# Keeping most nodes in place: a graph network's row permutation with four indirect transfers a batch in place of eight

## The chip, the cores and the metric

The kernel runs on one core of one Trainium2 chip. The metric is the device time of one execution in microseconds, the median of several runs. Engines are named as in the profile: PE (TensorE), PEld (its weight loads), DVE (VectorE), ACT (ScalarE), POOL (GpSimd), SP (SyncE, which here only issues DMAs, strictly in order).

## What is computed

Two layers on 16 batches of 1024 nodes with 128 features, and a 0/1 adjacency matrix per batch.

```
h = max(layernorm(x), 0)
x = x + layer0(h, adj)                       # masked dense attention
h = max(layernorm(x), 0)
x = x + layer1(h, adj, nodemask, ...)

layer0: v, q, k = relu(x W + b);  att = softmax(q k' masked by adj)
        relu(att v Wo + bo)
layer1: adj_d = dilate(adj)                  # sequential thinning of neighbours, node after node
        h1 = bn(relu(sage(h,  adj_d)))       # sage: deg-mean over adj_d, two matmuls, row norm
        h2 = bn(relu(sage(h1, adj_d)))       # bn: over all batches and nodes
        h3 = bn(relu(sage(h2, adj_d)))
        [h1, h2, h3] Wl + bl
```

After the thinning nearly all nodes have at most themselves or one neighbour left. The nodes with more to them are few: the "core" nodes (at most 128 a batch) keep a small matrix among themselves, the "special" ones (core included, at most 256) need a flag of their own. All other rows of adj_d are trivial.

## The kernel before, in words

The fast path (`fast`, L521) has five stages on one time line.

**Attention** (about 20 to 765 us). Sixteen steps of 48 ticks, one batch each; a tick is a third of a score block, and `pace` (L834) runs after each. Everything beside the score and value matmuls is written out by hand on the agenda (`plan_step`, L775): lists of tick numbers say when a generator's next piece is emitted. The pieces that matter here, by the step i in which they are emitted (list numbers of 48 and above fall into the following step):

- `load` (L158) for batch i+1: eight pairs, tile k at tick 1+6k. Each issues the DMA of 128 adjacency rows into one of three buffers `st` on SP and then ACT's exponential that reads them (L167); three ticks later ACT counts zeros (L184). The DMA and its reader are emitted at the same tick, so the lead that a load has over its use comes only from SP running ahead of the other engines, as far as free buffers allow.
- `load_x` (L666) at the start of step i brings x of batch i+2 into one of five buffers, the one that batch i-3 had. A column of the tile gets the node's number (L669).
- `sort` (L243) for a pair of batches in every odd step, ticks 27 to 36: it ranks core and special nodes and works out `slot` (a full permutation: core first, special next, then the rest) and `pick`.
- `gather` (L288): thirteen pieces a batch, for both batches of a pair, from tick 37 of the odd step to tick 46 of the next even one. Eight one-hot tiles, eight matmuls of one column (L300) for the core nodes' row numbers, then an indirect DMA of 128 adjacency rows on POOL (L305), a DVE scan over them (L309), and more.
- `norms_of_x2` (L706): the row norms of x after layer 0, ready around tick 22 of the second step after the batch's own; POOL writes the last of them (L586) into the x tile.
- `store` (L742): eight indirect DMAs of 128 rows of 524 bytes from POOL, which scatter x to `x2_d` in slot order, in the second step after the batch's own, ticks 27 to 41.

POOL further normalises x for the next projection (L592). In even steps that work and the newton steps of the norms stand ahead of the second batch's L305.

**Round one** (to 915 us): sage on the slot order. `load_x2` (L861) brings x2 back, POOL normalises (`enter`, L894), DVE solves the last four batches' thinning beside it. Batch 15's norms and store are emitted here.

**Round two** (to 990 us): sage again.

**Round three** (to 1119 us): sage, and the first two thirds of the last linear layer plus x2. The result rows of 11 of 16 batches have to go back from slot order to node order: `scatter_rows` (L1247) writes [h3 | z] with eight indirect DMAs of 1 KB rows to `y_d`, paced by `pace_scatters` (L1210), each behind a tiny POOL copy (L1217) that waits for recent DVE work; `load_back` (L1230) loads the rows three batches later. The other five (`STAY`) stay in slot order.

**The end** (from 1119 us): batch norm three, the last third (`final`, L1302), and the output: one dense store for the 11, eight indirect scatters (L1292) for each of the five.

All indirect DMAs are issued from POOL, all dense ones from SP. Each queue is in order, and a wait holds whatever is behind it.

## Time and profile before

| | us |
|---|---|
| median of 3 runs (1195.01 to 1197.49) | 1195.18 |
| the profiled execution | 1192.21 |
| its span, first to last instruction | 1190.4 |

| stretch, us | PE busy | DVE | ACT | POOL | DMA share | GB/s |
|---|---|---|---|---|---|---|
| 30 to 740, attention | 657.43 | 514.75 | 516.72 | 315.38 | 0.41 | 122 |
| 765 to 800, into round one | 25.30 | 22.15 | 13.81 | 25.70 | 0.40 | 107 |
| 800 to 915, round one | 85.84 | 99.72 | 66.45 | 64.97 | 0.18 | 48 |
| 915 to 990, round two | 64.77 | 62.27 | 51.60 | 5.99 | 0.05 | 12 |
| 990 to 1119, round three | 121.62 | 92.28 | 42.18 | 92.66 | 0.71 | 213 |
| 1119 to 1190.4, the end | 49.94 | 27.98 | 13.88 | 47.93 | 0.56 | 168 |

The DMA share is the mean busy share of the core's 16 DMA engines; it can exceed 1 where packets overlap. In attention, odd steps take 43.5 to 45.3 us with 0 to 0.8 us of PE idle (from step 3 on), even ones 47 to 53 us with 4.6 to 7.8.

| DMA | issues | median us from issue to landing |
|---|---|---|
| adjacency tile to `st`, SP | 128 | 3.6 |
| x tile, SP | 16 | 4.5 |
| x2 back, SP, round one / round three | 16 / 16 | 4.0 / 6.2 |
| x2 scatter, POOL | 128 | 2.8 |
| y scatter, POOL | 88 | 3.5 |
| adjacency rows gather, POOL | 16 | 4.6 |
| y back, SP | 22 | 5.8 |
| out, dense, SP | 11 | 4.0 |
| out, scatter, POOL | 40 | 2.4 |

### The profile page before, as it was taken

The numbers are of one execution on the slowest core, as the hardware profiler recorded it, in microseconds if no ns is written. First come the engines' busy times: TensorE is split into PE (matmuls) and PEld (weight loads), VectorE is DVE, ScalarE is ACT, GpSimd is POOL, SyncE is SP. The second block draws the span as 40 slices with busy tenths as digits, with TensorE's granted clock in tenths as the row PEclk, the third lists the DMA queues.
The fourth block names the chain that finished last, engine by engine and source line by source line (L and its number), as shares of the span: only waits on it lengthen the run. The fifth ranks groups of instructions, "written<-read, shape, count | busy, mean of one in ns | idle before, by whom it ended". The sixth has DMA issues, their size and how long they took to land.

```text
span 1190.4 us, 22335 instructions
## 1 busy us (share of the span) xinstructions
PE 1049.6 (88%) x7693; PEld 815.7 (69%) x7723; DVE 860.0 (72%) x2627; ACT 727.7 (61%) x1658; POOL 566.7 (48%) x1063
## 2 busy tenths in 40 slices
PE   7799899899889989989989989878876997999794
PEld 3567677667667666757656657667765997999784
DVE  6767656677777767867867877868887886777742
ACT  5578688677768868767767765246654772333221
POOL 0320743644445346356165270589740101878775
PEclk9999999999999999999999999989899998999897
DMA  6544345344344443543424431243300002788764
GB/s 212 159 130 142 103 129 149 107 127 143 102 121 113 150 124 96 159 124 104 146 87 130 139 104 24 58 109 86 96 1 1 1 1 74 237 246 248 219 195 132
DMA packets 135340, 143.78 MB, mean 121 GB/s; under 512 B 25904, under 2 KB 111280, under 8 KB 135216
## 3 DMA queue, kind: packets, MB, share of 16 engines
q1 hardware_dynamic: 123312, 111.10, 32.5%
q0 software_dynamic: 11904, 31.15, 8.0%
q8 instruction: 63, 1.03, 0.4%
q14 instruction: 61, 0.50, 0.1%
HBM read 113.71 MB, written 28.51 MB: 119 GB/s over the span
## 4 chain that ended last, share of the span: by engine, by line
PE 50%; DVE 22%; POOL 8%; ACT 7%; DMA 6%; issue 5%; POOLq 0%; SPq 0%; DVEq 0%; ACTq 0%
PE ps L714 11%; PE po L730 10%; PE pm L693 6%; PE po L1000 5%; DMA rows<-in_adj_dram,row 4%; DVE e L717 4%; PE pt L1058 2%; DVE left L309 2%; PE ph L1242 2%; ACT e L716 2%; PE pd L193 2%; PE ph L1243 2%; DVE m L366 2%; PE pm L701 2%; POOL out_dram L548 2%
## 5 line engine op out<-in xcount | busy, mean ns | idle before, releaser
L730 PEld LDWEIGHTS po<-vw,e 128*128 128x128 f32 x2048 | 271.8, 193 | 64.9 <-issue 64.5
L730 PE MATMUL po<-vw,e 128*128 128x129 f32 x2048 | 305.6, 283 | 0.0
L714 PE MATMUL ps<-qT,kT 128*128 128x512 f32 x512 | 270.0, 610 | 0.8 <-ACT e L716 0.8
L717 DVE TENSOR_TENSOR e<-e,ab 128x512 f32<-128x512 f32 x256 | 177.4, 694 | 120.7 <-ACT e L716 119.3
L716 ACT ACTIVATE e<-ps 128x512 f32<-128x512 f32 x256 | 152.8, 597 | 102.3 <-PE ps L714 78.5
L548 POOL DMA_INDIRECT x_d<-xt,slot x128 | 143.1, 1118 | 38.3 <-issue 34.9
L167 ACT ACTIVATE ab<-st,d_one_k 128x1024 bf16<-128x1024 f32 x128 | 146.9, 1148 | 1.2 <-DMA st<-in_adj_dram 1.2
L580 POOL TENSOR_SCALAR ln_t<-ln_st 128x8 f32<-128x8 f32 x31 | 7.7, 248 | 289.9 <-DVE ln_st L573 234.6
L184 ACT ACTIVATE junk<-st 128x1024 bf16<-128x1024 f32 x112 | 118.2, 1056 | 0.0
L548 POOL DMA_INDIRECT y_d<-y,nodes x88 | 86.3, 981 | 18.1 <-issue 13.3
L739 ACT ACTIVATE o<-po,recips 128x128 f32<-128x128 f32 x128 | 46.7, 367 | 77.2 <-DVE recips L737 77.2
L1016 ACT ACTIVATE sq<-po 128x512 f32<-128x512 f32 x64 | 38.1, 597 | 78.1 <-PE po L1035 43.5
L714 PEld LDWEIGHTS ps<-qT,kT 128*128 128x128 f32 x512 | 78.4, 192 | 7.5 <-issue 3.1
L592 POOL TENSOR_SCALAR hn<-xt,ln 128x128 f32<-128x128 f32 x120 | 73.8, 626 | 1.6
L309 DVE TENSOR_TENSOR_SCAN left<-rows 128x1024 f16<-128x1024 f32 x16 | 36.6, 2289 | 46.4 <-DMA rows<-in_adj_dram,row 46.4
L199 DVE SCALAR_TENSOR_TENSOR junkv<-pd,ab 128x64 bf16<-128x64 int32 (+7 forms) x128 | 57.6, 450 | 15.1 <-PE pd L193 15.0
L1000 PE MATMUL po<-ws,r 128*128 128x128 f32 x512 | 68.3, 278 | 0.0
L237 PEld LDWEIGHTS <-ab 128*128 128x128 bf16 x448 | 26.4, 97 | 60.7 <-issue 60.1
L592 POOL TENSOR_SCALAR hn<-xt 128x128 f32<-128x128 f32 x112 | 57.0, 518 | 22.7 <-PE pt L602 21.8
L1000 PEld LDWEIGHTS po<-ws,r 128*128 128x128 f32 x512 | 65.6, 195 | 1.1
L1019 DVE TENSOR_REDUCE nrm<-sq 128x4 f32<-128x512 f32 x64 | 43.5, 681 | 22.4 <-ACT sq L1016 22.1
L305 POOL DMA_INDIRECT rows<-in_adj_dram,row x16 | 17.1, 1068 | 83.0 <-DVE row L303 56.5
(330 smaller groups left out, 2414.0 us busy)
## 6 DMA issues: line engine op xcount, KB each, us to landing
st<-in_adj_dram SPq DMA_DIRECT2D x128, 512.0 KB, 3.6
r<-y_d SPq DMA_DIRECT2D x22, 512.0 KB, 5.8
xt<-x_d SPq DMA_DIRECT2D x16, 524.0 KB, 4.0
xt<-in_x_dram SPq DMA_DIRECT2D x16, 512.0 KB, 4.5
x<-x_d SPq DMA_DIRECT2D x16, 512.0 KB, 6.2
out_dram<-r SPq DMA_DIRECT2D x11, 512.0 KB, 4.0
x_d<-xt,slot POOLq DMA_INDIRECT x128, 2.8
y_d<-y,nodes POOLq DMA_INDIRECT x88, 3.5
```

Source lines behind the costliest of these rows:

```text
L167: nc.scalar.activation(ab[:, k, :], st, AF.Exp, bias=self.one_k, scale=ONE_K, accum_out=self.deg[:, b, k:k + 1])
L184: nc.scalar.activation(junk(), st, AF.Exp, scale=-ZERO_K, accum_out=zeros)
L199: nc.vector.scalar_tensor_tensor(junk.rearrange("p a b -> p (a b)")[:, :n], pt.rearrange("p a b -> p (a b)").bitcast(I32)[:, :n], 1.0, ab[ ...
L309: nc.vector.tensor_tensor_scan(left[:, ::-1], rows[:, ::-1], rows[:, ::-1], 0.0, op0=OP.add, op1=OP.bypass)
L548: d = nc.gpsimd.indirect_dma_start(out=dst, out_offset=bass.IndirectOffsetOnAxis(ap=slots, axis=0), in_=src, in_offset=None)
L592: engine.tensor_scalar(hn[:, k, :], xt[:, k, :D], minus[:, k // 2, k % 2, None], rstd[:, k // 2, k % 2, None], op0=OP.add, op1=OP.mult)
L693: nc.tensor.matmul(pp, w, hT[:, 512 * g:512 * g + 512], start=True, stop=True)
L714: nc.tensor.matmul(p, K[b][:, k * P:(k + 1) * P], Q[b][:, c], start=True, stop=True)
L716: later(1, lambda: nc.scalar.activation(e, p, AF.Exp))
L717: later(2, lambda: nc.vector.tensor_mul(e, e, AB_[b][:, k, c]))
L730: nc.tensor.matmul(po[:, q % 2, :], E[k][:, i * P:(i + 1) * P], V[b][:, k, :], start=(k == 0), stop=(k == NB - 1))
L1000: nc.tensor.matmul(po[:, i, :], hT[:, c:c + P], wxk, start=(i == 3), stop=False)
```

## The change

Slots are assigned anew. Core and special nodes still occupy the first slots of the first two blocks (256 slots). A node that is neither stays where it is, except where its own place in the first two blocks is needed: such a displaced node goes to the place that a special node from further behind has left. Blocks 2 to 7 are then nearly the natural order.

- `sort` computes `pick` for 256 slots, and for the displaced nodes of the first two blocks whom they change with; twelve small operations of that run on POOL.
- `gather` computes the node numbers of all 256 slots: the eight matmuls have 256 columns, and four DVE operations read their columns out.
- `store` becomes a dense DMA of the tile in node order (SP), two indirect fetches of the 256 special rows from there, two indirect scatters of the displaced rows of blocks 0 and 1 (POOL), and a dense DMA of the fetched rows over the first two blocks (SP). The node number column is gone.
- Round three sends batches 0 to 8 home: a dense store of y (SP), two fetches by `slot`, two scatters by `source` (POOL), and two loads of blocks 2 to 7 (SP). x2 is loaded into the y tile, which now has four buffers. The paced copies are gone.
- The end takes the seven batches 9 to 15 first, which are still in slot order: each a dense store to `y_d` and one to `out` (blocks 2 to 7), two fetches, two scatters of special rows to `out`, a dense store of blocks 0 and 1. Batches 0 to 8 follow with one dense store each. Three batches are transposed and raised before the last batch norm, not one.

```diff
-STAY = (2, 5, 8, 11, 14)
+HOME = 9
-XW = D + 3
+XW = D + 2
...
         nc.tensor.matmul(pp[:, 1, :, :, 0], self.onesb, count, start=True, stop=True)
+        for k in range(2):
+            nc.tensor.matmul(pp[:, 1, :, :, 1], self.onesb, kind[:, :, :, k], start=(k == 0), stop=(k == 1))
         yield
...
+        g = nc.gpsimd
+        g.tensor_sub(gone, other, stays)
...
+        g.tensor_mul(skip, skip, self.spare[:, None, :].to_broadcast([P, 2, 2]))
+        self.displaced[b0] = with_, where
         yield
...
-        pi = self.bank([P, 1], F32)
+        ph = self.bank([P, S], F32)
         for k in range(NB):
-            nc.tensor.matmul(pi, onehot[:, k, :P], self.node16[:, k:k + 1], start=(k == 0), stop=(k == NB - 1))
+            nc.tensor.matmul(ph, self.node16[:, k:k + 1].to_broadcast([P, P]), onehot[:, k, :],
+                             start=(k == 0), stop=(k == NB - 1))
         yield
+        def column(i):
+            nc.vector.scalar_tensor_tensor(line[:, :P], ph[:, i * P:(i + 1) * P], 1.0, self.identf, op0=OP.mult,
+                                           op1=OP.mult, accum_out=home[:, i:i + 1])
+        column(0)
         row = self.pool.tile([P, 1], I32, name="row")
...
         nc.gpsimd.indirect_dma_start(out=rows, out_offset=None, in_=self.adj.rearrange("b n m -> (b n) m"),
                                      in_offset=bass.IndirectOffsetOnAxis(ap=row[:, 0:1], axis=0))
+        column(1)
+        with_, where = (t[:, b % 2] for t in self.displaced[b - b % 2])
+        for k in range(2):
+            nc.vector.scalar_tensor_tensor(line, self.iota, with_[:, k:k + 1], ph, op0=OP.is_equal, op1=OP.mult,
+                                           accum_out=home[:, 2 + k:3 + k])
...
         def store(b):
-            for k in range(NB):
-                scatter(x2_d[b], dil.slot[:, b, k:k + 1], X[b][:, k, :], f"x2_{b}")
+            natural = x2_d[b][:N].rearrange("(k p) d -> p k d", p=P)
+            nc.sync.dma_start(natural, X[b])
+            yield
+            special = dpool.tile([P, 2, XW], F32, name="special")
+            for k in range(2):
+                fetch(special[:, k, :], x2_d[b][:N], source[:, b, k:k + 1])
                 yield
+            for k in range(2):
+                scatter(x2_d[b], away_to[:, b, k:k + 1], X[b][:, k, :], f"x2_{b}")
+                yield
+            nc.sync.dma_start(natural[:, :2, :], special)
             X.pop(b)
+            yield
...
-        AT_STORE = every(75, NB, 2)
+        AT_STORE = [78, 84, 85, 91, 92, 95]
-        LAST_NORMS, LAST_STORE = [42, 44, 46, 48, 50], every(54, NB, 2)
+        LAST_NORMS, LAST_STORE = [42, 44, 46, 48, 50], [53, 58, 59, 64, 65, 68]
...
+            def send_home(b, y):
+                there = y_d[b].rearrange("(k p) d -> p k d", p=P)
+                put(2, lambda: nc.sync.dma_start(there, y))
+                for k, to in enumerate((tall(b), r1[b // 2][:, b % 2, :])):
+                    put(7 + k, lambda k=k, to=to: fetch(to[:, :2 * D], y_d[b], slot[:, b, k:k + 1]))
+                    put(12 + k, lambda k=k: scatter(y_d[b], source[:, b, k:k + 1], y[:, k, :], f"y_{b}"))
+                def back():
+                    for i, rows in enumerate((rows_r, rows_z)):
+                        nc.sync.dma_start(rows(b)[:, 2:, :], there[:, 2:, i * D:i * D + D])
+                put(19, back)
...
+        def send_out(b):
+            there = y_d[b].rearrange("(k p) d -> p k d", p=P)
+            rows = rows_z(b)
+            def dense():
+                nc.sync.dma_start(there, rows)
+                leave(nc.sync.dma_start(places[b][:, 2:, :], rows[:, 2:, :]), b)
...
+            put(2, dense)
+            for k in range(2):
+                put(6 + k, lambda k=k: fetch(rows_r(b)[:, k, :], y_d[b], slot[:, b, k:k + 1]))
+                put(8 + k, lambda k=k: special(k))
+            put(13, lambda: leave(nc.sync.dma_start(places[b][:, :2, :], rows_r(b)[:, :2, :]), b))
...
-        order = [b for i in range(0, B - 1, 3) for b in (i + 2, i, i + 1)] + [B - 1]
+        order = list(range(HOME, B)) + list(range(HOME))
```

`put(n, fn)` runs `fn` n ticks later, where a round-three batch has eight ticks and a batch of the end four. `fetch` is an indirect DMA on POOL that reads rows by number.

## The prediction

> **What bounds the kernel now.** I read the slices first, then the waits by engine, then single stretches in order of time.
>
> ```profile
> PE   7799899899889989989989989878876997999794
> POOL 0320743644445346356165270589740101878775
> DMA  6544345344344443543424431243300002788764
> ...
> L548 POOL DMA_INDIRECT x_d<-xt,slot x128 | 143.1, 1118 | 38.3 <-issue 34.9
> ```
>
> A slice is 29.8 us. PE is full for 25 slices (attention and dilation, 30 to 740 us: PE 657 of 710), POOL only in round three and the end (last seven digits). So the scatters that the change thins out in attention (L548, 143.1 us) stand on an engine with room; their saving is worth nothing there unless somebody waits for POOL.
>
> What does matter there is the order of the SP queue:
>
> ```profile
> SPq L166 <- ACT junk L184: 338.6, 79, 8.1
> SPq L668 <- DMA x_d<-xt,slot: 149.4, 30, 18.9
> ```
>
> SP stands still most of the time: for a free adjacency buffer (L166) and, at each step's end, for the last scatter, so that the next x can be loaded (L668). It is in order; whatever is put between waits like these delays all loads after it. One pair of steps (i = 8, 393.1 to 440.5 us, and i = 9, to 484.1), SP, POOL, ACT and PE in turn:
>
> ```profile
> 405.82 0.33 SPq L166 DMA_DIRECT2D st<-in_adj_dram  x1
> 474.48 0.38 SPq L668 DMA_DIRECT2D xt<-in_x_dram  x1
> 475.59 2.16 SPq L166 DMA_DIRECT2D st<-in_adj_dram  x2
> ...
> 415.61 0.21 POOL L586 TENSOR_TENSOR xt<-ln_t 128x8 f32<-128x8 f32 x1
> 418.22 1.06 POOL L305 DMA_INDIRECT rows<-in_adj_dram,row  x1 [0.15 <-issue]
> 461.60 0.22 POOL L586 TENSOR_TENSOR xt<-ln_t 128x8 f32<-128x8 f32 x1
> ...
> 415.63 1.14 ACT L167 ACTIVATE ab<-st,d_one_k 128x1024 bf16<-128x1024 f32 x1
> 484.06 1.15 ACT L167 ACTIVATE ab<-st,d_one_k 128x1024 bf16<-128x1024 f32 x1
> ...
> 416.83 1.62 PE L602 MATMUL pm<-identf,hn 128*128 128x128 f32 x4 [1.00 <-POOL hn L592]
> 428.98 1.13 PE L693 MATMUL pm<-hT,w_L_gnn_Wk 128*128 128x512 f32 x2 [1.95 <-ACT qT L694]
> ```
>
> The load of tile k=5 leaves at 405.82, ten us ahead of its use (ACT, 415.63); tile k=0 of the next batch leaves at 475.59, 8.5 us ahead (484.06). L586 on xt (415.8, 461.8) is when the row norms that are stored with x are ready.
>
> The end is POOL's:
>
> ```profile
> 1131.44 0.95 POOL L548 DMA_INDIRECT out_dram<-r,nodes  x1 [0.30 <-issue]
> ...
> 1180.67 0.96 POOL L548 DMA_INDIRECT out_dram<-r,nodes  x1 [0.30 <-issue]
> ```
>
> Forty scatters without a gap, (1180.67-1131.44)/39 = 1.262 us each; PE is done at 1174.1. The last lands about 2.4 us after its issue (median of that row), 1183.1; the rest to 1190.4 is the closing.
>
> **A: the dense store of x, middle of an even step.** It stands at tick 30, right before the load of k=5 (tick 31), and needs the norms. In step 8 it can leave at 415.8 only, so k=5 leaves at 416.2 and not at 405.8. In front of it are 532 KB: at 300 GB/s (round three moved 213 GB/s at a DMA share of 0.71) 1.8 us. An adjacency load lands in 3.6 us, so k=5 lands at 421.6, and ACT holds from 415.6: 6 us, with the exps, the hT and qT evictions behind it, and PE behind these. But PE and DVE already stand there for the rows gather (418.22, landed 422.8, DVE idle 6.24 us before its scan); I follow ACT's list after the hold (hT, e, junk, qT: 4 us) and it is through at about 426, when today's o eviction starts (426.1). What is left is the rows' own delay: 512 KB that now share the engines with the store and three loads let go at once, at most 1.6 us at half rate (0.52 MB at E's 320 GB/s); 1.3, because its first part goes before them. Ends: 0 and 5.7 a step. I take 1.3, seven even steps: **+9**.
>
> **B: the start of the step after an odd one.** The chain is now dense store, two fetches, two scatters, each behind the landing of the one before. Store 461.8, landed 466.5. But on POOL the new sort's 12 small operations (tick 33) come ahead of the fetches (tick 36); their inputs come from DVE at about 470.5 (the operations they replace end at 470.0), and at 0.28 us each (0.20 and a gap of 0.08, the ln_t rows) they end at 474. Fetches 474 and 475.3; landed 2.8 later (median of x_d), 478; scatters 478 and 479.3, landed 482.2. Today the last scatter lands at 474.4. SP holds the patch of 133 KB, the load of x, the diagonal and k=0 until then: 8 us later, against a lead of 8.5 of which the landing behind the x load takes some 5.5. ACT is held 4 to 5 us. Scores stop two PSUM buffers later, so I count 2.5 (ends 0 and 5.4). Leads of the five such loads are 8.4 to 10.1; the sixth (12.6) has room: **+12.5**. In even steps POOL has nothing between, and the chain ends at about 429, earlier than today's 432.8.
>
> **C: PE and DVE in the gather.** Eight 128x1 matmuls (L300, 0.18 us together) become eight 128x256 (L324's shape, 0.87): +0.69. In even steps PE idles 4.6 to 7.8 us anyway; odd steps have at most 0.8 of idle, so seven times 0.69: **+5**. The four new DVE operations (dg's row, 0.34 and 0.08 for 128x128; twice that at most for 256) are 0.4 ahead of the rows gather and 1.7 behind it, hidden in DVE's wait for the rows, in odd steps in B's hold; without that cover 1.7 x 16 = 27.
>
> **D: into round one.** load_x2(2) left at 761.1; it now stands behind batch 14's store (norms at 778.6) and its patch. The chain of B from 778.7: landed 783, fetched by 787, scatters landed at 791.5. Then the load, 4.0 to landing: 795.5. On POOL two normalisations of batch 2 (L592, 791.69) come before batch 15's rows gather, at 792.73 today, then at 796.7: 4 us later on the chain that leads through DVE. Ends 0 and 4.3; I take **+3.5**. Thinner POOL work in round one (four transfers fewer, no node numbers, L898 0.24 each) hides behind PE and DVE; so does L669's copy (0.17) that falls away in attention.
>
> **E: round three.** 88 scatters (1.36 us with their mark) become 36 indirect transfers; POOL goes free. That gives 1.6 us: turns follow each other at 7.33 us, fourteen of them from 1008.49 would end at 1111.1 and end at 1112.70. Against that, a home batch now moves 0.5 MB (x2), 1.05 (y out), 0.26 + 0.26 and 0.79 (back): 2.88 MB, nine in a row; at 320 GB/s (what loaded stretches of eight us show) 9.0 us against PE's 7.33. Before it was 2.62 MB in two batches of three. The four y buffers come free when the scatters land, and load_rows stands ahead of the next dense store in SP, so lateness adds up: 9 x 1.7 = 15, less some 5 of slack in the early loads, less the 1.6. Ends -1.6 and +13; I take **+6**.
>
> **F: the end.** Three raises before the last batchnorm put four more evictions (0.6 us each) ahead of its Sqrt: +1.3. First dense store about 1130.7, landed 1134.8; then POOL 28 x 1.262 = 35.4 us. The last fetch starts at 1166.4 and lands at 1169. PE is done earlier (two raises fewer after the norm and four moved ahead), at about 1170, but SP's order puts batch 15's patch before the out stores of the last seven natural batches; they leave in a burst: 3.8 MB at 300 GB/s, 12.7 us, and about 2 more to land: 1184.5 against 1183.1. Ends -8 (no hold: last store 1171, landed 1175) and +5: **+1.5**.
>
> Sum: 9 + 12.5 + 5 + 3.5 + 6 + 1.5 = 37.5. The profiled execution took 1192.2 (span 1190.4), 3.0 below the median 1195.2, so 1229.7 for such an execution and 1195.2 + 37.5 = 1232.7 for the median, **1232** in round numbers.
>
> The Trainium skill speaks against the plan on one point: DMA: Bandwidth & Descriptors, "Issuing engines are not separate DMA queues", says that DMAs of all issuers run on the same 16 engines and that another issuer saves sequencer time alone. Round three's rows agree (share over 1 with both queues at work), and by the rule E would be its upper end. The page's "Anatomy of one DMA" (told there for GpSimd's path) puts a DMA at 2.0 us and bytes over 436e3; as an estimate the dense store of B would land after 3.2 us, not 4.7, which would make B's hold 1.5 us shorter and the sum some 5 us less.
>
> **Rivals.** R1, faster: the end alone counts. If SP's new waits stay inside the loads' lead (A, B, D at 0) and batch 15's patch isn't waited for long (F -8), with E at -1.6: 1195.2 - 9.6 = 1185.6. For it: loads lead by 10 to 20 us in most places, and POOL's gapless end. Against it: the two leads above are the short ones, and the patch is in order. It decides if k=5 lands before 416 and k=0 before 484. R2, attention absorbs, the rest costs: C, E, F and a third of A and B: 5 + 6 + 1.5 + 7 = 1215. R3, holds paid nearly in full: A 4 and B 5 a time, D 4, E 10, C, F: 28 + 25 + 4 + 10 + 5 + 2 = 1269. That it doesn't do what it says: the transfers are written out one by one, I give it nothing.
>
> **Chances.** Forecast 0.55 (own range 1222 to 1245), R2 0.20, R3 0.12, R1 0.13. 1192 to 1264 leaves R1 and half of R3 out. 0.2% is what a measurement of this kernel can tell from no change. Faster 0.13, same 0.04 (between R1 and R2), slower 0.83.
>
> **What would show it.** ACT's L167 idle before, by st's landing, where it is 7.9 us in all today: about 60. Steps after odd ones longer by 3 to 5. rows of batch 15 at 797. PE idle in round three's first nine batches. SP's last out stores in a burst behind a fetch. Wrong if the steps keep their 43.5 and 47 to 53 us.

## The result and the profile after

| | before | after |
|---|---|---|
| median, us (same chip, 4 runs each) | 1195.1 | 1296.02 |
| ratio after to before (95% interval) | | 1.0843 [1.0821, 1.0865] |
| span of the profiled execution, us | 1190.4 | 1295.0 |
| start to the first bn_aggr (attention, dilation, round one) | 915.6 | 991.5 |
| round two | 73.5 | 73.4 |
| round three | 130.9 | 156.5 |
| the end | 70.4 | 73.6 |

Slower, as predicted, but by 101 us and not by 37, beyond the range's 1264. The spans of the two profiled executions differ by 104.6: 75.9 of it up to the end of round one, 25.6 in round three, 3.2 in the end. (The borders are the three starts of DVE's bn_aggr, one a batch norm.)

The slices of the changed kernel's page, 32.4 us each:

```profile
PE   7899798898899799889789889857876979878792
PEclk9999899999999899889889989978998999988996
DMA  7534435335333443353433441143500014888077
```

PE is no longer full in attention, and the granted clock (PEclk) falls below 9 in 9 of its first 28 slices, where that of the kernel before does in one. The DMA row has hardly changed: attention has not become a matter of bytes alone.

The waits by engine of the changed kernel (sum in us, times, longest):

```profile
ACT ab L171 <- DMA st<-in_adj_dram: 84.9, 19, 8.1
...
DVE left L354 <- DMA rows<-in_adj_dram,row: 78.6, 8, 13.9
...
SPq L807 <- DMA x_d<-xt,moves: 208.8, 16, 19.5
SPq L798 <- DVE xt L630: 159.1, 13, 27.3
SPq L170 <- ACT junk L188: 147.2, 39, 8.0
```

In this row ACT's wait for adjacency tiles was 1.2 us before (the prediction's 7.9 has the first tile of the kernel in it, 6.7). SP used to stand for free buffers, ahead of everybody (L166, 338.6); now it stands in front of the patch (L807, the dense DMA that puts the fetched rows into the first two blocks) and the dense store (L798), with the loads behind it. DVE's wait for the gathered rows went from 46.4 to 78.6.

One even step (i = 8, 423.4 to 475.5 us), SP, ACT and PE in turn:

```profile
415.59 0.38 SPq L807 DMA_DIRECT2D x_d<-special  x1
416.02 0.72 SPq L722 DMA_DIRECT2D xt<-in_x_dram  x1
...
417.78 11.83 SPq L170 DMA_DIRECT2D st<-in_adj_dram  x5
...
446.22 0.38 SPq L798 DMA_DIRECT2D x_d<-xt  x1
446.70 2.20 SPq L170 DMA_DIRECT2D st<-in_adj_dram  x3
...
423.36 1.15 ACT L171 ACTIVATE ab<-st,d_one_k 128x1024 bf16<-128x1024 f32 x1 [4.77 <-DMA st<-in_adj_dram]
...
452.60 1.15 ACT L171 ACTIVATE ab<-st,d_one_k 128x1024 bf16<-128x1024 f32 x1 [6.02 <-DMA st<-in_adj_dram]
...
425.14 2.07 PE L767 MATMUL ps<-qT,kT 128*128 128x512 f32 x2 [3.81 <-ACT e L769]
454.38 1.67 PE L746 MATMUL pm<-hT,w_L_gnn_Wq 128*128 128x512 f32 x2 [3.54 <-ACT hT L657]
```

At its start the patch lets go of SP at 415.6, the load of k=0 goes at 417.8, ACT stands 4.77 us for it (this is B), PE 3.81 for ACT's e. In its middle the dense store waits for the norms until 446.2, k=5 goes half a us later, ACT stands 6.02 (this is A) and PE 3.54 for ACT's hT, the transposed h that ACT brings out of PSUM for the next projection.

In the table, steps run from ACT's L171 (L167 before) on k=0 of one batch to that of the next; "even" is the sum of steps 2, 4 to 12, "odd" of 3, 5 to 13. Since B delays that mark itself, the two columns share B between them, and their sum is the safe number.

| kernel | even | odd | PE idle in both | clock, even | step 14 to bn_aggr | time | ratio to before |
|---|---|---|---|---|---|---|---|
| before | 297.1 | 265.1 | 36.7 | 0.983 | 240.2 | 1195 | |
| after | 317.1 | 309.2 | 68.2 | 0.907 | 250.8 | 1296.0 | 1.0843 |
| b_dense | 324.3 | 267.4 | 52.9 | 0.947 | 244.5 | 1226.9 | 1.0258 [1.0223, 1.0292] |
| b_small | 312.9 | 264.5 | 41.9 | 0.951 | 242.5 | 1213.2 | 1.0143 [1.0109, 1.0177] |
| b_wide | 303.2 | 268.8 | 30.8 | 0.949 | 242.8 | 1204.8 | 1.0070 [1.0042, 1.0099] |
| a_late | 303.6 | 306.8 | 56.2 | 0.916 | 249.8 | 1285.7 | 1.0772 [1.0717, 1.0826] |
| a_patch | 324.9 | 272.9 | 50.2 | 0.942 | 251.9 | 1272.8 | 1.0629 [1.0592, 1.0667] |
| a_warm | 328.6 | 272.3 | 44.1 | 0.964 | 255.3 | 1277.0 | 1.0683 [1.0643, 1.0722] |
| a_x2early | 314.6 | 309.0 | 67.9 | 0.918 | 246.1 | 1291.6 | 1.0795 [1.0751, 1.0839] |
| a_three | 311.5 | 272.3 | 41.5 | 0.951 | 249.1 | 1261.5 | 1.0564 [1.0527, 1.0601] |
| a_six | 312.4 | 273.1 | 43.3 | 0.956 | 245.0 | 1229.6 | 1.0299 [1.0254, 1.0343] |

Clock is the granted clock as a share of full speed. Times are medians of several runs, stages those of one execution each, and these vary: seven executions with the changed kernel's attention untouched reached the first bn_aggr between 988.9 and 996.4 us, and six with its round three untouched took 152.9 to 160.0 us there. A smaller difference in one stage of one execution is no finding by itself.

### The profile page after: what moved, and what is told of

The parts are those of the page before. It is cut to its first block, busy times and chain, and to the rows that moved or that the text cites. A ratio compares the mean times of both kernels' runs of the same rounds, so it can differ in the third digit from the quotient of the medians.

```text
span 1295.0 us, 22232 instructions
## 1 busy us (share of the span) xinstructions
PE 1090.6 (84%) x7693; PEld 839.9 (65%) x7723; DVE 881.5 (68%) x2758; ACT 723.5 (56%) x1654; POOL 447.0 (35%) x957
## 3 DMA queue, kind: packets, MB, share of 16 engines
q8 instruction: 62, 1.02, 0.3%
## 5 line engine op out<-in xcount | busy, mean ns | idle before, releaser
L783 PEld LDWEIGHTS po<-vw,e 128*128 128x128 f32 x2048 | 280.1, 199 | 72.3 <-issue 71.6
L783 PE MATMUL po<-vw,e 128*128 128x129 f32 x2048 | 313.8, 288 | 0.1
L767 PE MATMUL ps<-qT,kT 128*128 128x512 f32 x512 | 278.5, 628 | 28.8 <-ACT e L769 28.8
L171 ACT ACTIVATE ab<-st,d_one_k 128x1024 bf16<-128x1024 f32 x128 | 147.1, 1149 | 84.9 <-DMA st<-in_adj_dram 84.9
L767 PEld LDWEIGHTS ps<-qT,kT 128*128 128x128 f32 x512 | 81.6, 200 | 36.8 <-ACT e L769 32.0
L354 DVE TENSOR_TENSOR_SCAN left<-rows 128x1024 f16<-128x1024 f32 x16 | 36.8, 2302 | 78.6 <-DMA rows<-in_adj_dram,row 78.6
L646 POOL TENSOR_SCALAR hn<-xt,ln 128x128 f32<-128x128 f32 x120 | 73.5, 626 | 1.6
L600 POOL DMA_INDIRECT r<-y_d,moves x32 | 31.2, 975 | 114.1 <-DVE r L1136 52.3
L1301 PE MATMUL ph<-ws,r 128*128 128x128 f32 x256 | 54.1, 295 | 5.3 <-DVE y L1136 2.8
L746 PE MATMUL pm<-hT,w_L_gnn_Wq 128*128 128x512 f32 x60 | 37.2, 705 | 24.9 <-ACT hT L657 24.9
L593 POOL DMA_INDIRECT x_d<-xt,moves x32 | 39.7, 1239 | 49.6 <-DMA special<-x_d,source 42.0
```

Of the source, the lines that this page charges most:

```text
L171: nc.scalar.activation(ab[:, k, :], st, AF.Exp, bias=self.one_k, scale=ONE_K, accum_out=self.deg[:, b, k:k + 1])
L593: d = nc.gpsimd.indirect_dma_start(out=dst, out_offset=bass.IndirectOffsetOnAxis(ap=slots, axis=0), in_=src, in_offset=None)
L646: engine.tensor_scalar(hn[:, k, :], xt[:, k, :D], minus[:, k // 2, k % 2, None], rstd[:, k // 2, k % 2, None], op0=OP.add, op1=OP.mult)
L767: nc.tensor.matmul(p, K[b][:, k * P:(k + 1) * P], Q[b][:, c], start=True, stop=True)
L783: nc.tensor.matmul(po[:, q % 2, :], E[k][:, i * P:(i + 1) * P], V[b][:, k, :], start=(k == 0), stop=(k == NB - 1))
L1301: nc.tensor.matmul(pz[:, i, :], r1[b // 2][:, b % 2, c], wl0, start=True, stop=False)
```

## The experiments

### Attention: each cost alone, on the kernel before

**b_dense**, A alone:

```diff
...
+        def dense(b):
+            nc.sync.dma_start(x3_d[b].rearrange("(k p) d -> p k d", p=P), X[b])
+            yield
...
                 plan(store(i - 1), start, LAST_STORE if last else AT_STORE)
+                if not last:
+                    plan(dense(i - 1), start, [78])
```

> The kernel before, with A alone: one dense store of x with its norms (520 KB) on SP at the changed kernel's place (tick 78 of its store's step, right before the load of k=5), into a buffer that nothing reads; the eight scatters stay. Theory 1 (the order of SP's queue holds the adjacency loads, and the whole hold reaches PE): ACT's ab idle by the landing of st rises from 8 us to 40 or more, at k=5 of the even steps, even steps are longer by about 3.3 each, odd ones by at most 0.5, time 1195 + 23 = 1218. Rival (the hold is hidden in the wait for the rows gather, as the prediction had it): ACT's idle rises as much, but the steps lengthen by 1.3 at most, time 1200 to 1204. Rival 2 (it is the bytes, not the order): odd steps lengthen as much as even ones.

Measured 30 us, of it 27.2 in the six even steps and 2.3 in the odd ones: one DMA costs three times the nine that the prediction gave it, and more than the 23 that theory 1 expected. (The eight scatters stay here, so its 520 KB come on top of what the kernel before moves.) Its waits:

```profile
DVE left L309 <- DMA rows<-in_adj_dram,row: 77.8, 9, 12.5
...
ACT ab L167 <- DMA st<-in_adj_dram: 59.5, 14, 8.5
...
PE pm L694 <- ACT hT L604: 25.9, 7, 4.4
```

The last line is the one that the prediction had ruled out: PE's projection of the next batch waits for ACT's hT, which stands behind the held ab. The kernel before has no such row. Two causes are mixed here, ACT's hold and the rows that land late.

**b_small** takes them apart: the same place in the queue, 65 KB.

```diff
...
-            nc.sync.dma_start(x3_d[b].rearrange("(k p) d -> p k d", p=P), X[b])
+            nc.sync.dma_start(x3_d[b], X[b][:, 0, :])
```

> The kernel before with b_dense's extra store cut to one of eight row groups (65 KB in place of 520), at the same place of SP's queue and behind the same norms, into a buffer that nothing reads. Order theory (the loads behind it are let go late, ACT is held): ab's idle stays at 50 or more us, time 1195 + 25 = 1220, as b_dense's 1227. Bytes theory (520 KB beside the rows gather and three loads make all of them land late): the wait of DVE for the rows falls from 78 back to 46 or so, time 1195 to 1206.

```profile
DVE left L309 <- DMA rows<-in_adj_dram,row: 66.4, 9, 11.0
...
ACT ab L167 <- DMA st<-in_adj_dram: 40.2, 8, 7.4
...
PE pm L694 <- ACT hT L604: 16.7, 7, 3.3
```

Between the two theories: 17 us with an eighth of the bytes. At this place in the queue 17 of A's 30 come with a store of any size, and 13 with the rest of the 520 KB.

**b_wide**, C alone:

```diff
-        pi = self.bank([P, 1], F32)
+        ph = self.bank([P, S], F32)
...
-            nc.tensor.matmul(pi, onehot[:, k, :P], self.node16[:, k:k + 1], start=(k == 0), stop=(k == NB - 1))
+            nc.tensor.matmul(ph, self.node16[:, k:k + 1].to_broadcast([P, P]), onehot[:, k, :],
+                             start=(k == 0), stop=(k == NB - 1))
...
```

> The kernel before, with C alone: in each of the 16 gathers eight matmuls 128x256 in place of eight 128x1, and DVE's diagonal read ahead of the rows gather and three reads behind it, whose results beyond the row are not used. Prediction's C: 7 x 0.69 = +5, time 1200. Rival (cover is gone, since DVE's 1.7 us behind the gather and a later row count in every step): 16 x (0.7 + 1.7) = +38, time 1233. Rival (all of it hidden): 1195.

Ratio 1.0070, 8.4 us: C was 5 in the prediction. The even steps, where it was to be hidden in PE's idle time, took 6.1 of the 9.8 in the table. PE's idle time there did fall (35.5 to 30.0 us), but its busy time rose by 11.6: 4.1 of work by the prediction's price (six times 0.69), the rest with a granted clock of 0.949 in place of 0.983.

### Attention: each cost taken away, on the changed kernel

**a_late**, the store of even steps behind k=6:

```diff
-        AT_STORE = [78, 84, 85, 91, 92, 95]
+        AT_STORE = ([78, 84, 85, 91, 92, 95], [86, 89, 90, 93, 94, 95])
...
-                plan(store(i - 1), start, LAST_STORE if last else AT_STORE)
+                plan(store(i - 1), start, LAST_STORE if last else AT_STORE[odd])
```

> The changed kernel, with the dense store of x in even steps moved from before the load of k=5 to behind that of k=6 (ticks 86, 89, 90, 93, 94, 95 in place of 78, 84, 85, 91, 92, 95); odd steps unchanged. Theory 1 (A is the order of SP's queue): the ab idle at k=5 of even steps (some 6 us each) goes, even steps are shorter by 3, time 1296 - 21 = 1275. Rival (A is the store's bytes beside the rows gather and the loads, wherever it stands): the idle moves to k=7 or into DVE's wait for the rows, time 1290 or more.

```profile
ACT ab L171 <- DMA st<-in_adj_dram: 41.6, 13, 7.6
...
DVE left L354 <- DMA rows<-in_adj_dram,row: 55.9, 8, 13.2
```

ACT's wait for st fell from 84.9 to 41.6 us, with no hold at k=5 of an even step left, DVE's wait for the rows from 78.6 to 55.9, PE's for hT from 24.9 to none; even steps fell by 13.5. The medians differ by 10, between the two theories, and their intervals touch, so the steps and waits carry this verdict: the place in the queue makes the hold, and neither wait that the rival expects has grown. Why no more than half of A's 30 came back stays open.

**a_patch**, patch and load of x later:

```diff
...
+            if i + 2 < B:
+                plan(load_x_later(i + 2), start, [10])
...
-            if i + 2 < B:
-                load_x(i + 2)
...
-        AT_STORE = [78, 84, 85, 91, 92, 95]
+        AT_STORE = ([78, 84, 85, 91, 92, 105], [78, 84, 85, 91, 92, 95])
```

> The changed kernel, with the patch of odd steps' stores moved behind the load of k=1 of the next step (tick 105 in place of 95), and every load of x from the step's first place to tick 10, behind it; even steps' stores unchanged. Theory 1 (B is SP held by patch and load of x until the late scatters have landed): the ab idle at k=0 (36 us in six steps) goes, odd steps are shorter by 4 to 5, time 1296 - 28 = 1268. Rival (the odd steps are long because POOL's chain makes the rows gather late, and ACT's hold at k=0 only covers DVE's wait for the rows): the idle at k=0 goes, but the odd steps stay within 1 us, time 1288 or more.

ACT's wait for st fell from 84.9 to 54.1 us (A's share is left), odd steps from 309.2 to 272.9 (before 265.1), both kinds together by 28.5 us, the time by 23. Theory 1 holds; which of the two that moved, the patch or the load of x behind it, costs how much isn't separated. POOL's chain of fetches and scatters is unchanged here, so it was not what made the odd steps long.

**a_warm** asks whether the low clock behind the stalls is a cost of its own (24 transposes more in even steps, on a_patch):

```diff
...
                 nc.tensor.transpose(pt[:, k, :], hn[:, 4 * g + k, :], identf)
+            for k in range(again if g else 0):
+                nc.tensor.transpose(pt[:, k % 4, :], hn[:, 4 * g + k % 4, :], identf)
```

> a_patch's kernel with 24 transposes more (4 us of PE, the same values written again) in each even step from step 2, right before the place where PE waits for ACT's hT (25.6 us in seven steps there, 4 each). Clock theory (a stall of 3.5 us or more lowers the granted clock for the 5 us behind it, and part of the loss is that): the wait is filled, PE's granted clock in even steps rises from 0.942 to 0.97 or more, even steps get shorter by 1 to 2 each although PE does 28 us more, time 1273 - 9 = 1264. Rival (the lower clock is no consequence of the stall, or the work takes as much as the clock gives): 1273 or more.

```profile
439.23 2.78 PE L658 MATMUL pm<-identf,hn 128*128 128x128 f32 x24
445.30 1.12 PE L752 MATMUL pm<-hT,w_L_gnn_Wq 128*128 128x512 f32 x2 [1.26 <-ACT hT L659]
```

The stall before Wq shrank to 1.26 us here (all seven from 25.6 to 5.1), the clock of even steps rose from 0.942 to 0.964, and no time came of it: 1277.0 against 1272.8. The rival stands. In four of the seven steps PE still waited for hT behind the extra work, so there ACT set the step and not PE's speed; in the other three the extra work may have taken what the clock gave.

**a_x2early** tests D:

```diff
-    load_x2(2)
...
+        load_x2(2)
         bias0 = pieces("pc0", bs[0], work)
```

> The changed kernel, with load_x2(2) in front of the transition (ahead of batch 14's dense store and patch on SP's queue) in place of behind it. Prediction's D (load_x2(2) behind the patch makes the normalization of batch 2, and behind it on POOL the rows gather of batch 15, late): rows of batch 15 go 4 to 8 us earlier than 129 us after the start of step 14, the first bn_aggr too, time 1296 - 6 = 1290. Rival (the rows gather of batch 15 is late because POOL's fetches and scatters stand ahead of it): 1295 or more.

POOL's timeline of the changed kernel, then of a_x2early:

```profile
868.65 0.88 POOL L646 TENSOR_SCALAR hn<-xt 128x128 f32<-128x128 f32 x2 [6.27 <-DMA xt<-x_d]
869.70 1.03 POOL L342 DMA_INDIRECT rows<-in_adj_dram,row  x1 [0.16 <-issue]
```

```profile
857.31 0.98 POOL L593 DMA_INDIRECT x_d<-xt,moves  x1 [0.30 <-issue]
860.73 1.03 POOL L342 DMA_INDIRECT rows<-in_adj_dram,row  x1 [0.16 <-issue]
```

After step 14's start the rows of batch 15 go at 129.0 us in the changed kernel (740.7 is that start), at 123.3 here (737.4), at 117.3 before. D's mechanism is half of the delay, 5.7 of 11.7; the rest is POOL's chain of batch 14, later (its norms 4.5 us) and longer than priced. The time's interval overlaps the changed kernel's, so D rests on these rows, and on this: from step 14 to the bn_aggr the five kernels with this edit take 244.5 to 246.2 us, all changed kernels without it 249.0 or more.

### Round three and the end

| kernel | round three | the end | time | ratio to before |
|---|---|---|---|---|
| before | 130.9 | 70.4 | 1195 | |
| after | 156.5 | 73.6 | 1296.0 | 1.0843 |
| a_spread | 142.9 | 91.7 | 1298.2 | 1.0861 [1.0819, 1.0904] |
| a_noback | 152.2 | 73.2 | 1291.9 | 1.0810 [1.0762, 1.0858] |
| a_noind | 128.2 | 74.5 | 1269.6 | 1.0624 [1.0559, 1.0689] |
| a_loadafter | 151.4 | 74.2 | 1290.6 | 1.0789 [1.0731, 1.0848] |
| a_copy | 145.8 | 72.9 | 1282.7 | 1.0721 [1.0687, 1.0755] |
| a_end | 160.0 | 66.2 | 1287.8 | 1.0767 [1.0723, 1.0812] |
| a_five | 145.7 | 65.9 | 1236.5 | 1.0353 [1.0296, 1.0409] |
| a_six | 138.6 | 66.0 | 1229.6 | 1.0299 [1.0254, 1.0343] |

**a_noback** and **a_noind** leave work out:

```diff
-                put(19, back)
```

> The changed kernel without the loads back of the nine home batches (2 x 384 KB each, 27% of their bytes); the end then reads rows that have not been put home. Bytes theory: the period of a home batch falls by the same share, from some 11 us to 8, round three by 20 us or more. Loop theory (dense store landed, fetches landed, scatters landed, next load, with two batches in it): the loads back stand outside the loop, and it gets shorter only by what the other landings gain from an emptier queue: period 9 to 10, round three shorter by 8 to 14.

```diff
-                for k, to in enumerate((tall(b), r1[b // 2][:, b % 2, :])):
-                    put(7 + k, lambda k=k, to=to: fetch(to[:, :2 * D], y_d[b], slot[:, b, k:k + 1]))
-                    put(12 + k, lambda k=k: scatter(y_d[b], source[:, b, k:k + 1], y[:, k, :], f"y_{b}"))
```

> The changed kernel without the two fetches and two scatters of the nine home batches (0.52 of 2.88 MB each, 18%); the first two row groups of these batches then hold other rows. Loop theory: the loop loses the two fetches' and scatters' issues and landings, some 8 of 21 us, the home batches run at PE's 7.33 us, and round three takes 131 us or less. Bytes theory: the period falls from some 11 us to 9, round three to some 140.

Without 27% of the bytes round three gains 4.3 us, less than either theory gave it and hardly outside the spread named above; without the chain of fetches and scatters 28.3, more than all it had lost, as the loop theory has it. The windows (busy us of PE, PEld, DVE, ACT, POOL, then clock, DMA share, GB/s) of the changed kernel, then of a_noind:

```profile
1100.00:1120.00 20.00, 19.04 (x161) 18.55 (x163) 14.27 (x30) 6.68 (x17) 7.25 (x8) 1.00 0.91 277
1120.00:1140.00 20.00, 14.60 (x109) 13.72 (x109) 9.09 (x20) 4.55 (x11) 6.54 (x7) 0.91 0.91 277
1140.00:1160.00 20.00, 13.34 (x111) 12.63 (x111) 7.38 (x15) 4.26 (x9) 7.87 (x8) 0.95 0.75 215
```

```profile
1100.00:1120.00 20.00, 20.00 (x176) 19.77 (x176) 14.61 (x30) 6.83 (x15) 0.00 (x0) 1.00 1.01 294
1120.00:1140.00 20.00, 20.00 (x176) 19.77 (x175) 15.07 (x31) 6.63 (x16) 0.00 (x0) 1.00 1.08 326
```

PE is full at 326 GB/s in the one and 13 to 15 of 20 us busy at 215 to 277 GB/s in the other. The changed kernel does not run into the engines' rate; it waits. For what, SP's and POOL's timelines show:

```profile
1109.38 0.36 SPq L1293 DMA_DIRECT2D y<-x_d  x1
1109.84 0.53 SPq L1309 DMA_DIRECT2D y_d<-y  x1
...
1118.37 0.98 POOL L600 DMA_INDIRECT r<-y_d,moves  x1 [4.54 <-PE ph L1302]
...
1123.33 1.00 POOL L593 DMA_INDIRECT y_d<-y,source  x1 [2.71 <-issue]
1124.63 0.99 POOL L593 DMA_INDIRECT y_d<-y,source  x1 [0.30 <-issue]
...
1131.31 0.36 SPq L1293 DMA_DIRECT2D y<-x_d  x1
1131.71 0.58 SPq L1309 DMA_DIRECT2D y_d<-y  x1
```

The dense store of 1109.84 lands, is fetched from at 1118, scattered to at 1123; when that has landed the load (L1293) at 1131.31 gets the buffer, and the next batch but one's store stands behind it in the queue. That is 21.5 us from store to load, for two batches.

**a_loadafter** puts the load behind the store:

```diff
-                    later(2, lambda b=b: load_rows(b + 1))
+                    put(3, lambda b=b: load_rows(b + 1))
```

> The changed kernel, with one line's place changed in round three: the load of the next batch's x2 into its Y buffer (L1293) goes onto SP's queue behind the dense store of the batch before (tick 3) and not ahead of it (tick 2). The same bytes, transfers, buffers and order of batches. Order theory (the dense store stands in SP's queue behind a load that waits for the scatters of an earlier batch, so only two batches are on their way home at a time, 21 us for two): the store leaves when its rows are ready, three batches are on their way, the period of the nine falls from some 11 us to 7.3 to 9, round three from 156.5 to 131 to 142, time 1296 - 20 = 1276. Latency theory (four Y buffers and 21 us from store to load are the limit, whatever the order): period stays at 10 or more, time 1290 or more.

The order theory falls: round three gains 5 us and not 14 to 25, the time no more than its interval leaves open. The loads of this kernel:

```profile
1121.50 0.47 SPq L1293 DMA_DIRECT2D y<-x_d  x1
...
1131.71 0.48 SPq L1293 DMA_DIRECT2D y<-x_d  x1
...
1161.42 0.49 SPq L1293 DMA_DIRECT2D y<-x_d  x1
```

Four loads further is the same buffer: 39.9 us for one round of it (x2 in, computed, stored, fetched, scattered), with four buffers 10 us a batch, whatever stands first.

**a_copy** shortens the round (on a_loadafter): the scattered rows are copied away, a buffer is free when its store has landed.

```diff
                 put(2, lambda: nc.sync.dma_start(there, y))
+                keep = tall(b)[:, 4 * D:].rearrange("p (k d) -> p k d", d=2 * D)
+                put(3, lambda: nc.gpsimd.tensor_copy(keep, y[:, :2, :]))
...
-                    put(12 + k, lambda k=k: scatter(y_d[b], source[:, b, k:k + 1], y[:, k, :], f"y_{b}"))
+                    put(12 + k, lambda k=k: scatter(y_d[b], source[:, b, k:k + 1], keep[:, k, :], f"y_{b}"))
...
-                put(19, back)
+                put(27, back)
```

> The changed kernel with a_loadafter's edit, and in round three the two row groups that are scattered are copied by POOL into the batch's free rows of r2 (128x512 floats) and scattered from there, so that a Y buffer comes free when its dense store has landed; the loads back go at 27 ticks, not 19. Latency theory (a buffer's round, load to next load, is 40 us, of which fetches and scatters take some 16; four buffers make 10 us a batch): the round falls to 25 us, PE sets the pace again, round three 130 to 138 in place of 156.5 (a_loadafter 151.4), time 1296 - 22 = 1274. Bytes theory (2.88 MB a home batch at 277 to 320 GB/s): 9 to 10 us a home batch as now, round three 146 or more.

```profile
1100.00:1120.00 20.00, 18.91 (x161) 18.45 (x162) 12.66 (x26) 6.57 (x15) 9.18 (x10) 1.00 0.97 304
1120.00:1140.00 20.00, 15.67 (x127) 14.97 (x129) 11.47 (x24) 5.15 (x12) 9.13 (x10) 0.97 0.95 289
1140.00:1160.00 20.00, 19.90 (x150) 19.74 (x153) 13.70 (x29) 6.04 (x15) 9.14 (x10) 0.86 1.02 309
```

The bytes theory's number came: 145.8. The DMA share is now 0.95 to 1.02 at 289 to 309 GB/s, and round three is 14.9 us longer than before, near the prediction's nine times 1.7. So of the 25.6 us 10.7 are the round of the buffers (give or take 3.5, by that spread) and 14.9 are left. That these are the bytes of nine home batches in a row is argued, not shown: a_noind has such a share with PE full. At PE's 7.33 us a batch 2.88 MB would need 393 GB/s, though, and no window here shows more than 326. **a_spread** spreads the nine:

```diff
...
-            for b in range(B):
-                if 0 < b < B - 1:
-                    later(2, lambda b=b: load_rows(b + 1))
+            turns = [0, 9, 1, 10, 2, 11, 3, 12, 4, 13, 5, 14, 6, 15, 7, 8]
+            for n, b in enumerate(turns):
+                if 0 < n < B - 1:
+                    later(2, lambda n=n: load_rows(turns[n + 1]))
```

> The changed kernel, with round three's batches in the order 0, 9, 1, 10, 2, 11, 3, 12, 4, 13, 5, 14, 6, 15, 7, 8, so that a home batch and a late one take turns; bytes and transfers stay. Both theories of round three's 25.6 us (bytes of nine home batches in a row; a loop of dense store, fetches, scatters and the next load, which holds two batches at a time) expect most of it back: round three 125 to 132 us against 156.5, time 1296 - 28 = 1268. Rival (the stall comes from somewhere else than the row of nine, as the rows that two batches share): no change, 1290 or more.

A miss: round three gained 13.6 us, half of what was expected, and the end lost 18.1. With home batches last, the tiles raised before the last batch norm lie in memory that the Y buffers have not yet given back:

```profile
ACT hT L1359 <- DMA y_d<-y,source: 9.9, 2, 8.5
```

ACT's hT stands another 9.4 us there with no releaser in the profile.

**a_end**, the patches last:

```diff
-            put(13, lambda: leave(nc.sync.dma_start(places[b][:, :2, :], rows_r(b)[:, :2, :]), b))
+            put(60, lambda: leave(nc.sync.dma_start(places[b][:, :2, :], rows_r(b)[:, :2, :]), b))
```

> The changed kernel, with the seven patches of the end (L1385) behind the nine home batches' out stores on SP's queue (60 ticks after their batch, not 13). Prediction's F (the patch of batch 15 waits for its fetches and holds the last seven out stores, 3.8 MB in a burst): the out stores leave from their final on, the last transfer lands at about 1281 in place of 1291, time 1296 - 9 = 1287. Rival (the end is the DMA engines' bytes or POOL's 28 transfers, the order costs nothing): 1293 or more.

The changed kernel's end has the burst behind the last patch that F foresaw; in a_end, whose end begins 8 us later, the same stores start 13 us earlier:

```profile
1275.34 0.37 SPq L1385 DMA_DIRECT2D out_dram<-r  x1
1275.81 10.34 SPq L1409 DMA_DIRECT2D out_dram<-r  x7
```

```profile
1262.68 16.78 SPq L1409 DMA_DIRECT2D out_dram<-r  x8
```

The end fell from 73.6 to 66.2 us, the time by 8, against 9 expected.

### Together

**a_three** (a_late, a_patch, a_spread), **a_five** (a_late, a_patch, a_loadafter, a_end, a_x2early and the order 0, 9, 1, 2, 10, 3, 4, 11, 5, 6, 12, 7, 8, 13, 14, 15), **a_six** (a_five and a_copy) have no edits of their own.

> The changed kernel with a_late's, a_patch's and a_spread's edits together. If A, B and E are separate and each is the order of a queue: even steps (2 to 12) 300 us, odd ones (3 to 13) 272, round three 128, time 1296 - 12 - 27 - 28 = 1229. Rival (they share a cause, the load on the DMA engines, and moving one only pushes the others): 1245 or more.

> The changed kernel with a_late's, a_patch's, a_loadafter's, a_end's and a_x2early's edits together, and the batches of round three in the order 0, 9, 1, 2, 10, 3, 4, 11, 5, 6, 12, 7, 8, 13, 14, 15 (no home batch among the last three). If each cause is the order of a queue and they are separate: first bn_aggr 945, round three 125, end 65, time 1295 - 86 = 1210, which leaves C and the slower matmuls of the even steps. Rival (in the end and in round three it is bytes and buffers): 1230 or more.

> a_five's kernel with a_copy's copy and later loads back. If the causes add up: first bn_aggr 947 as a_five, round three 132 in place of a_five's 145.7, end 66, time 1236 - 13 = 1223; it would still be slower than the kernel before, by C, the last batches of the dilation and what is left in the even steps. Rival (round three is limited by the bytes also when the home batches are spread): 1232 or more.

a_three missed by 32 and ended where its rival had it, 1245 or more: odd steps as expected, even ones 11 us longer than expected, round three 142.7 and not 128, and a_spread's longer end (89.8). a_five met its first bn_aggr (946.8) and its end (65.9) and missed by 26 through round three, 145.7 and not 125, where a_six's copy then brought 7. a_six, 1229.6, between its theories' 1223 and 1232, is the best of this change here and 3% slower than the kernel before. What it loses against before: 23 us in the steps (C takes 10 of them), 5 from step 14 on, 8 in round three; the end is 4 shorter. The other 13 in the steps and the 8 in round three, where the home batches are spread and the buffers' round is cut, are open: ACT waits 10.2 us for adjacency tiles in a_six (1.2 before), DVE 50.8 for the rows (46.4 before).

**a_seven** (with the load of x at tick 20) and **a_eight** (with a new order of the batches) go on from a_six:

```diff
-        AT_STORE = ([78, 84, 85, 91, 92, 105], [86, 89, 90, 93, 94, 95])
+        AT_STORE = ([78, 84, 85, 91, 92, 105], [92, 96, 97, 101, 102, 108])
```

> a_six's kernel with the even steps' dense store behind the load of k=7 (ticks 92, 96, 97, 101, 102, 108; the load of x at tick 20), so that it leaves after the rows gather has landed. If A's bytes count only beside the rows gather: DVE's wait for the rows falls, even steps (2 to 12) 303 in place of 312, time 1229.6 - 10 = 1220. Rival (the bytes are paid wherever they stand, or the late fetches and scatters now hold the odd step's gather): even and odd steps together no shorter, 1228 or more.

```diff
-HOME = 9
+HOME = 11
```

> a_six's kernel with eleven home batches in place of nine, in the order 0, 11, 1, 2, 3, 12, 4, 5, 6, 13, 7, 8, 9, 10, 14, 15. POOL's chain at the end loses 8 of 28 transfers (10 us), round three gets 5.8 MB more; if the end is still POOL's, the end falls from 66 to 58 and round three grows by 2 to 6 (three home batches in a row in three places): 1223 to 1228. Rival (the end is the DMA engines' out stores by now): the end stays at 64 or more, time 1230 or more.

These two ran on another chip, on which the kernel before took 1254.98 us (15 runs), 60 more than on the others: a_seven 1250.05, ratio 0.9954 [0.9931, 0.9977], a_eight 1245.83, 0.9934 [0.9908, 0.9959]. In the end of both, engines stand for up to 13.5 us for something that the trace does not name, as here:

```profile
DVE r L1139 <- remote: 24.1, 4, 11.3
```

So the two times say nothing of the other chips, and whether a_eight would beat the kernel before there is open. The stages ahead of that do: a_seven's even and odd steps are 309.5 and 272.7, 3 us less than a_six's, and DVE's wait for the rows, 50.4 us, is a_six's 50.8. So the later place brings nothing, as the rival's number has it. Its reason, that the 520 KB are paid wherever the store stands, is not shown: ACT waits 9.0 us for adjacency tiles here (1.2 before), and DVE's wait is near the 46.4 of before.

## Why the prediction was right in sign and wrong in size

| step | predicted | shown | by |
|---|---|---|---|
| A | 9 | 30 (17 place in the queue, 13 with the bytes there) | b_dense, b_small |
| B | 12.5 | 23 (time), 28.5 (steps) | a_patch |
| C | 5 | 8.4 | b_wide |
| D | 3.5 | 4.7, and 5.9 beside it | a_x2early, step 14 to bn_aggr |
| E | 6 | 25.6 (10.7 round of buffers, 14.9 argued to be bytes) | a_copy |
| F | 1.5 | 3.2 | the end, a_end |

The right column adds up to 101 to 106; the kernel lost 101. A and C were added to the kernel before, B and E taken out of the changed one, D and F read from stages, so that the sum comes out is no proof of each.

**Mechanisms.** All six are there, at the lines and in the direction named. A's holds were predicted as seven of 6 us; they are 6.1, 5.9, 5.4, 6.0, 7.0, 6.7 and 5.0. F's burst behind batch 15's patch is there, and without it the end is 7.4 shorter (rival R1's F: 8).

**A, the step that failed most in attention**, was this: "PE and DVE already stand there for the rows gather", with ACT's list "through at about 426" and only the rows' own delay left. It set the hold's price to nothing. DVE did stand, PE did not. In step 8 of the kernel before, from the issue of the rows gather to its landing:

```profile
418.20:422.80 4.60, 4.60 (x28) 3.08 (x29) 0.04 (x1) 2.87 (x5) 3.66 (x4) 1.00 0.47 145
```

PE (the first number behind the length) was busy for all of it, and among its work was the projection from hT. ACT's list holds hT, so the hold takes this work away: 25.9 us in seven stalls that the kernel before hasn't. With an eighth of the bytes the place in the queue still cost 17, seven steps together, where the prediction gave it nothing; the bytes, priced at 1.3 a step, made 13/7 = 1.9.

**B** had three errors. There were six holds, not five. They were longer (4.8 to 8.1, 36.3 us together, against 22.5): in step 9 the dense store (496.76, 21.3 us into the step) and the fetches (33.4) left as forecast, but the patch left 43.6 us into the step and not 41.7, since fetches and scatters took longer to land; and k=0's exponential began 7.4 to 9.2 us after the patch had left, where some 5.5 was taken for its landing. And half of each hold was written off because "scores stop two PSUM buffers later": of 36 us of hold 23 to 28 came back when it was removed.

**C** was mis-sized in even steps: part of PE's idle time covered it, and the rest of the gain went into a lower clock. Why the clock is lower there with less idle time stays open.

**D** was right as far as it goes (5.7 us earlier rows without it, 4.3 predicted at most); that the chain of batch 14 would begin 4.5 us late was left out.

**E** had the right two halves and priced one. "The four y buffers come free when the scatters land, and load_rows stands ahead of the next dense store" was written down, but its length was never added up: load about 5, batch, dense store 5 to 9, fetches 3 to 5, scatters up to 7.6 to land, 40 us for four buffers. Only bytes were priced, and 6 taken of their 13.

**Rivals.** The nearest was R3 at 1269, holds paid nearly in full: it has A 28, B 25, D 4, against 30, 23 and 5 shown; E (10) is what it lacks. The choice between forecast and R3 was made on cover that the trace does not show: a stall of PE that wasn't there, in work that the held engine was feeding.

The Trainium skill, DMA: Bandwidth & Descriptors, "Issuing engines are not separate DMA queues" (the DMAs of all issuers run on the same 16 engines), would have put E at its upper end, 13. a_copy's windows are in line with it (14.9 us at a DMA share of about 1), but the changed kernel lost 25.6. The estimate from that page's "Anatomy of one DMA", 3.2 us for the dense store of x, does not agree: the median landing in the changed kernel is 5.9. Nor would 1.5 us less there have shortened B, as the prediction says: by its own times the fetches wait until 474 for the new sort's operations, and the store has landed at 466.5.

## What to carry to other kernels

A DMA that waits for a late result belongs behind the loads in an in-order queue, not between them; one such store and one such patch with its load cost 40 us here (17 in b_small, 23 in a_patch), though SP stood still most of the time. When a hold is said to be hidden in another engine's wait, look whether that engine stands still there at all, and what feeds it: if it is the held engine, the hold is paid. For buffers that go through a chain of DMAs, add up the chain from load to next load and divide by the buffers before dividing bytes by a rate.

## What was not expected of the hardware

PE's granted clock falls behind each of the twelve stalls of 3.3 us or more in the changed kernel's steps 2 to 14. In step 8 (same columns as the windows above):

```profile
423.00:428.00 5.00, 2.86 (x7) 1.65 (x8) 2.05 (x3) 4.64 (x9) 0.00 (x0) 0.61 0.65 212
428.00:433.00 5.00, 5.00 (x28) 3.64 (x27) 2.76 (x9) 3.15 (x8) 0.00 (x0) 0.71 0.59 186
...
453.00:458.00 5.00, 3.62 (x12) 2.40 (x13) 0.32 (x1) 3.54 (x7) 1.51 (x2) 0.68 0.71 286
```

0.61 and 0.71 behind the stall at 425, 0.68 behind that at 454. The Trainium skill, TensorE: Matmul & The Clock Gate, "HAM oscillation — how this bites in real kernels", has it as a rule: a PE wait beyond about 3.4 us, and the clock goes to half (4/8). These rows agree, but the rule isn't all of it: behind a stall of 3.69 us a_patch has 1.00 (246 to 251 us), and the changed kernel has 0.50 at 553.9 to 557.2 us with no stall over 1.3 us in the 8 us before. Filling the stall (a_warm) brought some of the clock back and no time, so here the low clock goes with the loss; that it is a cause of it is not shown.

A scatter of 128 rows landed 2.5 us after its issue in a quiet moment of round three (1094.24 to 1096.70) and 7.6 us beside a 1 MB store and two loads of 384 KB (1111.54 to 1119.13). The same kernel can take 1195 to 1197 us on four chips and 1255 on a fifth.
